# Gated delta attention with a mixture of experts on one core: moments, gathers and running products traced earlier

## The chip, the cores and the metric

The kernel runs on one core of a Trainium2 chip. The metric is device time in microseconds of one execution, the median of several runs. The engines are named as in the profile: PE is TensorE, DVE is VectorE, ACT is ScalarE, POOL is GpSimd, and SP is SyncE, which here only issues DMAs.

## What is computed

The block normalises x and adds to it an attention layer and a mixture of experts. All numbers are float32; x has 2 batches of 2048 tokens of 512.

```python
xn = _layernorm(x)                                   # (2, 2048, 512)
# attention: 16 heads of 128
q, k, v = (silu(causal_dwconv(xn @ W, cw, cb)) for each of q, k, v)   # 4 taps, k scaled by 128 ** -0.5
alpha, beta = sigmoid(xn @ Wa + ba), sigmoid(xn @ Wb + bb)            # one per token and head
def step(S, qt, kt, vt, at, bt):                     # over the 2048 tokens
    err = S @ kt - vt
    S = at * S - bt * outer(err, kt)
    return S, S @ qt
attn = (norm_per_head(o) * ln_w + ln_b) * sigmoid(xn @ Wg) @ Wo
# experts: the first 512 tokens, each to 4 of 16, sorted by expert
ffn = scatter_add(w * (silu(xs @ gate) * (xs @ up)) @ down)
return x + attn + ffn
```

## The kernel before

The recurrence over tokens is done in chunks of C = 128 tokens. Inside a chunk the triangular system is solved with products of small matrices, and a state S of 128x128 per head goes from chunk to chunk. Four chunks make a block (BLK = 512 tokens, CB = 4); a batch has NBK = 4 blocks or NC = 16 chunks. Heads go in pairs (HG = 2), so a batch has NP = 8 pairs and the program 16 units u, each a pair of heads of one batch.

**Before the recurrences.** norm(b) takes x in four groups of four chunks. For a group it loads four tiles xin (four buffers), computes mean and variance on DVE (L370, L371), adds eps (ve, L373), and raises to the power -0.5 on POOL (rs, L375). Each chunk is then normalised on DVE (xn, L384), transposed on PE (L390), copied by ACT, and multiplied by the weights of alpha and beta (L393). At the end norm computes the decays and writes them to memory: a_d (alpha per token) and gin_d. norm(0) runs first, then route, which sorts the tokens by expert. The two first units' keys (keys(0), keys(1), called from firsts) follow, and between them the generator norm(1) is stepped once from the 13th step on, and projection(0) at steps 20, 23, 26 and 29.

**keys(u)** has eight items (four blocks of two heads) of two steps each, a step being what runs up to a yield. The first step projects (L149, four matmuls in one of two PSUM banks "p"), and convolves: ACT copies the bank (raw, L131) and forms the last tap with the bias (cv, L135), POOL copies three columns of halo (L130, L133), DVE adds three taps (L137), ACT applies Silu to give kf (L139). The second step multiplies each chunk of kf with itself (L201) into a bank (the bank "o" in firsts, a bank "p" in the recurrences), builds the decays decA with four ACT operations (L209), turns them into running products with a scan on DVE (L213) whose multiplier is row, the alphas of the item broadcast to all partitions by a DMA (ask, L182), and multiplies both (aTf, L215). The tile row has one buffer; the next item's is asked for behind aTf. The first row of a unit is asked for when keys(u) starts.

**inverses(u)** computes 32x32 inverses on POOL in 30 rounds of a product and a sum (L243, L246). For unit 0 it is drained at once, between keys(0) and keys(1); for later units a round is handed out at three of the six ticks.

**recurrence(b)** walks the 128 chunks of a batch, and two more steps to drain. A step m has six ticks. In each, before (chunk m: the inverse of 128x128), after (chunk m-1: the state) and output (chunk m-2) are stepped; projection of the next block (q, v, g) at ticks 1 and 4, keys(u + 2) at ticks 0 and 3, the experts at ticks 2 and 5:

```python
if tick in (1, 4):
    step(nxt)
if tick in (0, 3):
    step(ks)
step(last)
if tick in (2, 5):
    step(ex)
```

So a unit's keys fill eight of its sixteen steps. **experts** is one generator over 31 tiles of 128 tokens; its first step gathers tokens (xg) and three parts of weights (w) by indirect DMAs on POOL (L900), the next transposes xg on PE (L920) and copies it to xgT (L922).

**What sets the order.** The text gives the traced order. The framework's scheduler then places each instruction on its engine's queue by its own model of time, with the traced order as priority, and derives all waits. Two calls in keys (keep_in_program_order on the decays and on the scan) hold these behind what was traced before them on their engine. Tiles of one tag share a fixed number of buffers.

Of the kernel before, what the change touches and what calls it, by code (L numbers as in the profile page):

```python
# [7 lines left out]
F32 = mybir.dt.float32  # L8
I32 = mybir.dt.int32
AF = mybir.ActivationFunctionType  # L10
ALU = mybir.AluOpType
# [3 lines left out]
P = 128  # L15
NB, T, HID = 2, 2048, 512
# [7 lines left out]
HG = 2  # L24
# [18 lines left out]
def block_kernel(ctx, tc, x, wq, wk, wv, wg, wo, wa, wb, ba, bb, par, consts,  # L43
# [9 lines left out]
    def bank(pool, tag):  # L53
        return pool.tile([P, 512], F32, tag=tag, name=tag)
# [104 lines left out]
    def load_wk(u):  # L159
        if u < NB * NP and u not in wks:  # L160
            wks[u] = load_w(ap, "wk", wk, u % NP * HG, f"wk{u}")

    def keys(u, xts, bank_k=(ps_p, "p")):

        b, hp = divmod(u, NP)
        h0 = hp * HG
        load_wk(u)
        w = wks[u]
        if u == NP:
            bt[b] = beta_of()
            nc.sync.dma_start(out=bt[b], in_=bt_d)
        n = CB * DW

        def ask(blk, h):  # L180
            row = ap.tile([P, n], F32, tag="row", name="row")
            nc.sync.dma_start(  # L182
                out=row, in_=a_d[b][h0 + h, blk * n:(blk + 1) * n].partition_broadcast(P))
            return row

        row = ask(0, 0)
        for blk in range(NBK):
            xt = xts(b, blk)
            for h in range(HG):
                ps = proj(w, h, xt)  # L190
                kt = ap.tile([P, BLK], F32, tag="kf", name="kf", bufs=2)
                conv_silu(ps, 1, h0, h, blk, kt)
                if (blk, h) == (NBK - 1, HG - 1):
                    if u + 1 != NP + 2:
                        load_wk(u + 1)
                nc.sync.dma_start(out=k_d[u][blk][h], in_=kt)
                yield
                pk = bank(*bank_k)
                for c in range(CB):
                    a = kt[:, c * C:(c + 1) * C]  # L200
                    nc.tensor.matmul(pk[:, c * C:(c + 1) * C], lhsT=a, rhs=a, start=True, stop=True)  # L201
                aT = ap.tile([P, CB, C], F32, tag="aTf", name="aTf", bufs=2)

                dec = ap.tile([P, CB, DW], F32, tag="decA", name="decA", bufs=2)
                for c in range(CB):
                    ci = blk * CB + c
                    tc.keep_in_program_order(nc.scalar.activation(  # L209
                        dec[:, c, :], unit, AF.Identity, scale=bt[b][:, ci, h0 + h:h0 + h + 1]))  # L210
                flat = dec.rearrange("p c j -> p (c j)")
                tc.keep_in_program_order(
                    nc.vector.tensor_tensor_scan(flat, row, flat, 0.0, ALU.mult, ALU.add))  # L213
                nc.sync.dma_start(out=dec_d[b][hp][blk][:, h * n:(h + 1) * n], in_=flat)
                nc.vector.scalar_tensor_tensor(  # L215
                    aT, pk.rearrange("p (c j) -> p c j", c=CB), -1.0 / D, dec[:, :, 0:C],
                    ALU.mult, ALU.mult)
                if (blk, h) != (NBK - 1, HG - 1):
                    row = ask(blk + (h + 1) // HG, (h + 1) % HG)
                o = h * NC + blk * CB  # L220
                nc.sync.dma_start(out=aT_d[u][:, o:o + CB, :], in_=aT)
                yield
# [124 lines left out]
    with ExitStack() as es:  # L347
# [11 lines left out]
        np_ = es.enter_context(tc.tile_pool(name="norm", bufs=2))  # L359
        def norm(b):  # L360
            psg = bank(ps_l, "l")
            for g in range(NBK):
                xin = [np_.tile([P, HID], F32, tag="xin", name="xin", bufs=4) for _ in range(CB)]
                for i in range(CB):
                    c = g * CB + i
                    nc.sync.dma_start(out=xin[i], in_=x[b, c * C:(c + 1) * C, :])
                mv = np_.tile([P, CB, 2], F32, tag="mv", name="mv")
                for i in range(CB):
                    st = np_.tile([P, 6], F32, tag="st", name="st")
                    nc.vector.bn_stats(st, xin[i])  # L370
                    nc.vector.bn_aggr(mv[:, i, :], st)  # L371
                ve = np_.tile([P, CB], F32, tag="ve", name="ve")
                nc.vector.tensor_scalar(ve, mv[:, :, 1], EPS, None, ALU.add)  # L373
                rs = np_.tile([P, CB], F32, tag="rs", name="rs")
                nc.gpsimd.tensor_tensor(rs, ve, mhalf[:, 0:CB], ALU.pow)  # L375
                if b == 0:
                    xt = xT[b, g] = xp.tile(
                        [P, NKT, BLK], F32, tag="xT", name=f"xT{b}_{g}", bufs=NBK)
# [93 lines left out]

        def firsts():
            for u in range(2):
                for _ in keys(u, get_xT, (ps_o, "o")):
                    yield
                if u == 0:
                    drain(inverses(0))
                    yield

        f0, p0, n1 = firsts(), projection(0), norm(1)
        for i, _ in enumerate(f0):
            if i > 12:
                next(n1, None)
            if i in (20, 23, 26, 29):
                next(p0)
# [23 lines left out]
    for t in [*ops[0].values(), *ops[1].values(), *invs]:  # L510
        nc.gpsimd.memset(t, 0.0)
    ex = experts(nc, bank, ps_p, half, k2, ident, wrow, trow, xn_d, y_d, (ew0, ew1, ew2), (ewd0, ewd1))
    def before(n, c):

        u, blk = blocks[n]
# [153 lines left out]
    def recurrence(b, first):  # L669
# [21 lines left out]
        for m, at in enumerate([*steps, None, None]):  # L691
# [30 lines left out]
            for tick in range(6):  # L722
# [8 lines left out]
                if tick in (0, 3):  # L731
                    step(ks)
                step(last)
                if tick in (2, 5):
                    step(ex)
                if inv and at and ci > 0:
                    if tick == 1:
# [274 lines left out]
```

## Time and profile before

| | |
|---|---|
| median of 3 runs | 4071.16 us (4069.39 to 4077.14) |
| the profiled execution's own time | 4071.89 us |
| its span, first to last instruction | 4070.1 us |
| mean granted clock of PE | 0.988 |
| busy: PE, DVE, ACT, POOL | 3825.9, 2337.3, 1642.1, 1822.5 us |
| DVE waiting for rows (the scan, L213) | 9.2 us in 9 cases |
| mean of a scan, of aTf, of a power 128x4 | 1380, 681, 1072 ns |
| DMA, mean over the span | 133 GB/s |

The page has a line for each engine in 40 slices of about 102 us: a digit is the busy share in tenths. A view of waits has, for each engine and line, whom it waited for, the total, the number of cases and the longest. A line of a timeline has start, duration, engine, line of the source, operation, output and inputs with their form and the number of instructions merged, and in square brackets the idle time just before with what ended it. The busy time of PE is modelled, and a wait with several causes is put down to the last of them.

### The profile page before, as it was taken

The numbers are of one execution on the slowest core, as the hardware profiler recorded it, in microseconds if no ns is written. First come the engines' busy times: TensorE is split into PE (matmuls) and PEld (weight loads), VectorE is DVE, ScalarE is ACT, GpSimd is POOL, SyncE is SP. The second block draws the span as 40 slices with busy tenths as digits, with TensorE's granted clock in tenths as the row PEclk, the third lists the DMA queues.
The fourth block names the chain that finished last, engine by engine and source line by source line (L and its number), as shares of the span: only waits on it lengthen the run. The fifth ranks groups of instructions, "written<-read, shape, count | busy, mean of one in ns | idle before, by whom it ended". The sixth has DMA issues, their size and how long they took to land.

```text
span 4070.1 us, 58930 instructions
## 1 busy us (share of the span) xinstructions
PE 3825.9 (94%) x18046; PEld 2463.9 (61%) x18046; DVE 2337.3 (57%) x6132; ACT 1642.1 (40%) x4025; POOL 1822.5 (45%) x3496
## 2 busy tenths in 40 slices
PE   8679999999999999999989999999999999999999
PEld 6356666666666666666654456666666666666554
DVE  6555565564655557676751056767676767666321
ACT  3344344443444435454530044545454545444210
POOL 1436556464564645454550045455454545472100
PEclk9889999999999999999999999999999999999999
DMA  4555555455555454354564344334443434424322
GB/s 148 158 150 166 164 161 164 148 162 152 161 160 160 147 148 130 108 151 117 174 200 124 106 128 118 108 116 113 113 119 107 120 107 123 123 75 121 100 94 78
DMA packets 579705, 541.36 MB, mean 133 GB/s; under 512 B 354688, under 2 KB 421760, under 8 KB 574272
## 3 DMA queue, kind: packets, MB, share of 16 engines
q1 hardware_dynamic: 557280, 456.18, 38.2%
q0 software_dynamic: 22112, 81.41, 6.5%
q8 instruction: 147, 2.41, 0.2%
q14 instruction: 166, 1.36, 0.1%
HBM read 363.69 MB, written 173.67 MB: 132 GB/s over the span
## 4 chain that ended last, share of the span: by engine, by line
PE 45%; DVE 12%; POOL 6%; ACT 5%; issue 2%; DMA 1%; SPq 0%; POOLq 0%; ACTq 0%; DVEq 0%
PE p L149 20%; PE p L781 11%; DVE cv L137 7%; POOL rs L643 2%; ACT cv L135 2%; PE c L615 2%; PE c L606 2%; POOL qg L311 2%; PE l L536 1%; PE o L629 1%; PE c L596 1%; PE o L632 1%; ACT raw L131 1%; PE p L932 1%; DVE o L657 1%
## 5 line engine op out<-in xcount | busy, mean ns | idle before, releaser
L137 DVE SCALAR_TENSOR_TENSOR cv<-raw,prm,cv 128x512 f32<-128x512 f32 x1152 | 921.8, 800 | 307.4 <-ACT cv L135 289.2
L131 ACT COPY raw<-p 128x512 f32<-128x512 f32 x384 | 223.2, 581 | 784.0 <-PE p L149 762.5
L149 PE MATMUL p<-xT,wv 128*128 128x512 f32 x1024 | 480.3, 596 | 4.6 <-DVE xgT L922 4.5
L149 PE MATMUL p<-xT,wq 128*128 128x512 f32 x1024 | 476.5, 595 | 7.4 <-DVE aTf L215 5.1
L149 PE MATMUL p<-xT,wg 128*128 128x512 f32 x1024 | 473.5, 594 | 3.9 <-ACT cv L135 3.5
L781 PE MATMUL p<-wo,oTf 128*128 128x512 f32 x1024 | 455.0, 596 | 1.2 <-DMA oTf<-oT_d 1.1
L149 PE MATMUL p<-xT,wk 128*128 128x512 f32 x896 | 417.2, 604 | 36.8 <-DVE aTf L215 29.7
L657 DVE TENSOR_SCALAR o<-o,mv,rs 128x128 f32<-128x128 f32 x512 | 194.8, 404 | 237.7 <-POOL rs L643 237.7
L781 PEld LDWEIGHTS p<-wo,oTf 128*128 128x128 f32 x1024 | 191.2, 192 | 219.5 <-issue 216.5
L643 POOL TENSOR_TENSOR rs<-rs,mhalf 128x2 f32<-128x2 f32 x256 | 229.0, 894 | 203.2 <-DVE rs L642 196.0
L565 POOL COPY inv<-iT 32x32 f32<-32x32 f32 x512 | 137.7, 269 | 386.9 <-DVE top L560 254.9
L133 POOL COPY halo<-raw 128x3 f32<-128x3 f32 x288 | 70.7, 245 | 528.3 <-ACT raw L131 523.5
L135 ACT ACTIVATE cv<-p,prm 128x512 f32<-128x512 f32 x384 | 301.0, 784 | 0.2
L550 POOL TENSOR_TENSOR kg<-kv,gd 128x256 f32<-128x256 f32 x256 | 177.6, 694 | 274.3 <-ACT kv L548 268.3
L243 POOL TENSOR_TENSOR t<-Y 128x30 f32<-128x30 f32 (+14 forms) x480 | 278.0, 579 | 38.2 <-DMA dec_d<-decA 0.2
L246 POOL TENSOR_TENSOR Y<-Y,t 128x30 f32<-128x30 f32 (+14 forms) x480 | 276.0, 575 | 36.5
L149 PEld LDWEIGHTS p<-xT,wk 128*128 128x128 f32 x896 | 161.3, 192 | 193.8 <-issue 154.4
L559 DVE STREAM_TRANSPOSE iT<-l 128x32 f32<-128x32 f32 x256 | 55.4, 216 | 382.4 <-PE l L557 382.3
L149 PEld LDWEIGHTS p<-xT,wq 128*128 128x128 f32 x1024 | 179.2, 191 | 156.2 <-issue 147.6
L149 PEld LDWEIGHTS p<-xT,wg 128*128 128x128 f32 x1024 | 179.6, 191 | 155.5 <-issue 150.2
L149 PEld LDWEIGHTS p<-xT,wv 128*128 128x128 f32 x1024 | 178.2, 191 | 145.6 <-issue 139.7
L606 PEld LDWEIGHTS c<-r,inv 128*128 128x128 f32 x960 | 140.1, 191 | 148.3 <-issue 66.1
(176 smaller groups left out, 7423.4 us busy)
## 6 DMA issues: line engine op xcount, KB each, us to landing
row<-a_d SPq DMA_DIRECT2D x128, 258.0 KB
dec_d<-decA SPq DMA_DIRECT2D x128, 258.0 KB
decB<-dec_d SPq DMA_DIRECT2D x64, 516.0 KB
k_d<-kf SPq DMA_DIRECT2D x128, 256.0 KB
gin<-gin_d SPq DMA_DIRECT2D x128, 256.0 KB
k<-k_d SPq DMA_DIRECT2D x64, 512.0 KB
aT_d<-aTf SPq DMA_DIRECT2D x128, 256.0 KB
oT_d<-oT SPq DMA_DIRECT2D x256, 128.0 KB
```

Of the source, the lines that this page charges most:

```text
L131: nc.scalar.copy(raw[:, KS - 1:], ps)
L135: nc.scalar.activation(cv, ps, AF.Identity, bias=cbias(p, h0 + h), scale=tap(p, h0 + h, KS - 1))
L137: nc.vector.scalar_tensor_tensor(cv, raw[:, j:j + BLK], tap(p, h0 + h, j), cv, ALU.mult, ALU.add)
L149: nc.tensor.matmul(ps, lhsT=w[:, k, h * D:(h + 1) * D], rhs=xt[k], start=(k == 0), stop=(k == NKT - 1))
L243: nc.gpsimd.tensor_tensor(t, bass.AP(col.tensor, col.offset, [col.ap[0], (Q, j), (0, n)]), bass.AP(row.tensor, row.offset, [row.ap[0], (0, ...
L246: nc.gpsimd.tensor_tensor(Y[:, 0:j, j + 1:], Y[:, 0:j, j + 1:], t, ALU.add)
L550: nc.gpsimd.tensor_tensor(kg, kv[:, 0], bcast(gd1[b][:, ci, hs], D), ALU.mult)
L565: nc.gpsimd.tensor_copy(inv[0:Q, h, Q:2 * Q], iT[r + Q:r + 2 * Q])
L606: nc.tensor.matmul(pw[:, h * D:(h + 1) * D], lhsT=inv[:, h, :], rhs=r[:, h, :], start=True, stop=True)
L643: nc.gpsimd.tensor_tensor(rs, rs, mhalf[:, 0:HG], ALU.pow)
L657: nc.vector.tensor_scalar(o[:, h, :], po[:, h * D:(h + 1) * D], mv[:, h, 0:1], rs[:, h:h + 1], ALU.subtract, ALU.mult)
L781: nc.tensor.matmul(py, lhsT=oT[:, h, :], rhs=wos[h], start=(h == 0), stop=(h == H - 1))
```

## The change

It has four parts. (1) norm(1) computes the moments of all four groups ahead: firsts steps it at steps 1, 3, 5 and 7 as well, each time loading a group of x and taking its statistics; at step 13 one power of 16 columns gives all 16 chunks' factors, and the groups of x are loaded a second time to be normalised. norm(0) keeps its order. (2) The generator of the experts gets its first step right after the memsets ahead of the recurrences, and step m = 0 of each recurrence no longer steps it. (3) In keys the decays, the scan and their store move from the second step of an item to the end of the first, behind the convolution; the second step keeps the products and aTf. (4) The row of the next item is asked for right behind the scan, and the last item of a unit asks for the first row of the next unit; the very first is asked for ahead of keys(0).

```diff
@@ -160,6 +160,15 @@
         if u < NB * NP and u not in wks:
             wks[u] = load_w(ap, "wk", wk, u % NP * HG, f"wk{u}")
 
+    rows = {}
+
+    def ask(u, blk, h):
+        if u < NB * NP:
+            rows[u, blk, h] = row = ap.tile([P, CB * DW], F32, tag="row", name="row")
+            nc.sync.dma_start(
+                out=row, in_=a_d[u // NP][u % NP * HG + h, blk * CB * DW:(blk + 1) * CB * DW]
+                .partition_broadcast(P))
+
     def keys(u, xts, bank_k=(ps_p, "p")):
 
 
@@ -177,13 +186,6 @@
             nc.sync.dma_start(out=bt[b], in_=bt_d)
         n = CB * DW
 
-        def ask(blk, h):
-            row = ap.tile([P, n], F32, tag="row", name="row")
-            nc.sync.dma_start(
-                out=row, in_=a_d[b][h0 + h, blk * n:(blk + 1) * n].partition_broadcast(P))
-            return row
-
-        row = ask(0, 0)
         for blk in range(NBK):
             xt = xts(b, blk)
             for h in range(HG):
@@ -194,12 +196,6 @@
                     if u + 1 != NP + 2:
                         load_wk(u + 1)
                 nc.sync.dma_start(out=k_d[u][blk][h], in_=kt)
-                yield
-                pk = bank(*bank_k)
-                for c in range(CB):
-                    a = kt[:, c * C:(c + 1) * C]
-                    nc.tensor.matmul(pk[:, c * C:(c + 1) * C], lhsT=a, rhs=a, start=True, stop=True)
-                aT = ap.tile([P, CB, C], F32, tag="aTf", name="aTf", bufs=2)
 
 
 
@@ -210,13 +206,19 @@
                         dec[:, c, :], unit, AF.Identity, scale=bt[b][:, ci, h0 + h:h0 + h + 1]))
                 flat = dec.rearrange("p c j -> p (c j)")
                 tc.keep_in_program_order(
-                    nc.vector.tensor_tensor_scan(flat, row, flat, 0.0, ALU.mult, ALU.add))
+                    nc.vector.tensor_tensor_scan(flat, rows.pop((u, blk, h)), flat, 0.0, ALU.mult, ALU.add))
                 nc.sync.dma_start(out=dec_d[b][hp][blk][:, h * n:(h + 1) * n], in_=flat)
+                m = blk * HG + h + 1
+                ask(u + m // (NBK * HG), m // HG % NBK, m % HG)
+                yield
+                pk = bank(*bank_k)
+                for c in range(CB):
+                    a = kt[:, c * C:(c + 1) * C]
+                    nc.tensor.matmul(pk[:, c * C:(c + 1) * C], lhsT=a, rhs=a, start=True, stop=True)
+                aT = ap.tile([P, CB, C], F32, tag="aTf", name="aTf", bufs=2)
                 nc.vector.scalar_tensor_tensor(
                     aT, pk.rearrange("p (c j) -> p c j", c=CB), -1.0 / D, dec[:, :, 0:C],
                     ALU.mult, ALU.mult)
-                if (blk, h) != (NBK - 1, HG - 1):
-                    row = ask(blk + (h + 1) // HG, (h + 1) % HG)
                 o = h * NC + blk * CB
                 nc.sync.dma_start(out=aT_d[u][:, o:o + CB, :], in_=aT)
                 yield
@@ -359,20 +361,43 @@
         np_ = es.enter_context(tc.tile_pool(name="norm", bufs=2))
         def norm(b):
             psg = bank(ps_l, "l")
-            for g in range(NBK):
+
+            def moments(mv, xs):
+                for i, a in enumerate(xs):
+                    st = np_.tile([P, 6], F32, tag="st", name="st")
+                    nc.vector.bn_stats(st, a)
+                    nc.vector.bn_aggr(mv[:, i, :], st)
+
+            def power(mv, n):
+                ve = np_.tile([P, NC], F32, tag="ve", name="ve")
+                nc.vector.tensor_scalar(ve[:, 0:n], mv[:, :, 1], EPS, None, ALU.add)
+                rs = np_.tile([P, NC], F32, tag="rs", name="rs")
+                a = mhalf[:, 0:1]
+                nc.gpsimd.tensor_tensor(
+                    rs[:, 0:n], ve[:, 0:n], bass.AP(a.tensor, a.offset, [a.ap[0], (0, n)]), ALU.pow)
+                return rs
+
+            def load(g):
                 xin = [np_.tile([P, HID], F32, tag="xin", name="xin", bufs=4) for _ in range(CB)]
                 for i in range(CB):
                     c = g * CB + i
                     nc.sync.dma_start(out=xin[i], in_=x[b, c * C:(c + 1) * C, :])
-                mv = np_.tile([P, CB, 2], F32, tag="mv", name="mv")
-                for i in range(CB):
-                    st = np_.tile([P, 6], F32, tag="st", name="st")
-                    nc.vector.bn_stats(st, xin[i])
-                    nc.vector.bn_aggr(mv[:, i, :], st)
-                ve = np_.tile([P, CB], F32, tag="ve", name="ve")
-                nc.vector.tensor_scalar(ve, mv[:, :, 1], EPS, None, ALU.add)
-                rs = np_.tile([P, CB], F32, tag="rs", name="rs")
-                nc.gpsimd.tensor_tensor(rs, ve, mhalf[:, 0:CB], ALU.pow)
+                return xin
+
+            if b > 0:
+                mvs = np_.tile([P, NC, 2], F32, tag="mvs", name="mvs", bufs=1)
+                for g in range(NBK):
+                    moments(mvs[:, g * CB:(g + 1) * CB, :], load(g))
+                    yield
+                rss = power(mvs, NC)
+            for g in range(NBK):
+                xin = load(g)
+                if b == 0:
+                    mv = np_.tile([P, CB, 2], F32, tag="mv", name="mv")
+                    moments(mv, xin)
+                    rs = power(mv, CB)
+                else:
+                    mv, rs = (a[:, g * CB:(g + 1) * CB] for a in (mvs, rss))
                 if b == 0:
                     xt = xT[b, g] = xp.tile(
                         [P, NKT, BLK], F32, tag="xT", name=f"xT{b}_{g}", bufs=NBK)
@@ -472,6 +497,8 @@
 
         def firsts():
             for u in range(2):
+                if u == 0:
+                    ask(0, 0, 0)
                 for _ in keys(u, get_xT, (ps_o, "o")):
                     yield
                 if u == 0:
@@ -480,7 +507,7 @@
 
         f0, p0, n1 = firsts(), projection(0), norm(1)
         for i, _ in enumerate(f0):
-            if i > 12:
+            if i > 12 or i in (1, 3, 5, 7):
                 next(n1, None)
             if i in (20, 23, 26, 29):
                 next(p0)
@@ -510,6 +537,7 @@
     for t in [*ops[0].values(), *ops[1].values(), *invs]:
         nc.gpsimd.memset(t, 0.0)
     ex = experts(nc, bank, ps_p, half, k2, ident, wrow, trow, xn_d, y_d, (ew0, ew1, ew2), (ewd0, ewd1))
+    next(ex)
     def before(n, c):
 
         u, blk = blocks[n]
@@ -731,7 +759,7 @@
                 if tick in (0, 3):
                     step(ks)
                 step(last)
-                if tick in (2, 5):
+                if tick in (2, 5) and m != 0:
                     step(ex)
                 if inv and at and ci > 0:
                     if tick == 1:
```

## Prediction

> **What bounds it now.** I read the page first: its head, and the slices of part 2.
>
> ```profile
> span 4070.1 us, 58930 instructions
> PE 3825.9 (94%) x18046; PEld 2463.9 (61%) x18046; DVE 2337.3 (57%) x6132; ACT 1642.1 (40%) x4025; POOL 1822.5 (45%) x3496
> ...
> PE   8679999999999999999989999999999999999999
> ```
>
> TensorE (PE) is busy for 94%, so the most that better order can win is its idle time, 4070.1 - 3825.9 = 244 us. Four fifths of the run are nines; slices 1 to 3 (0 to 305 us) are not. The change moves no matmul out of the program, so I ask only which idle time it can fill. Next, the view of waits for PE, total us, times and longest:
>
> ```profile
> PE c L390 <- DVE xn L384: 44.3, 4, 25.2
> PE p L149 <- DVE aTf L215: 41.6, 43, 1.9
> ...
> PE p L920 <- DMA xg<-xn_d,trow: 10.8, 1, 10.8
> ...
> PE p L932 <- DVE aTf L215: 5.7, 8, 1.2
> ...
> PE o L201 <- DVE aTf L215: 4.8, 2, 3.2
> ...
> PE p L946 <- DVE aTf L215: 2.5, 3, 1.1
> ```
>
> Three causes, and the change touches each. The timeline of the 25.2 us wait (DVE, then POOL, then PE):
>
> ```profile
> 178.50 0.33 DVE L373 TENSOR_SCALAR ve<-mv 128x4 f32<-128x4 f32 x1
> 205.59 1.00 DVE L384 TENSOR_SCALAR xn<-xin,mv,rs 128x512 f32<-128x512 f32 x2 [26.75 <-POOL rs L375]
> ...
> 202.68 1.89 POOL L252 COPY X<-Y 128x1024 f32<-128x1024 f32 x1
> 204.53 1.02 POOL L375 TENSOR_TENSOR rs<-ve,mhalf 128x4 f32<-128x4 f32 x1
> ...
> 206.19 1.97 PE L390 MATMUL c<-unit,xn 128*128 128x128 f32 x8 [25.16 <-DVE xn L384]
> ```
>
> ve is ready at 178.8; its power of 1.02 us runs at 204.5, because POOL is inside the 60 operations of inverses(0) from 165.0 to 204.6. DVE holds at xn, and PE behind it. The third group's chunks are the victims. The steady stage, one step of the second recurrence:
>
> ```profile
> 2630.22 2.33 DVE L213 TENSOR_TENSOR_SCAN decA<-row,decA 128x516 f32<-128x516 f32 x1
> 2633.09 0.41 DVE L657 TENSOR_SCALAR o<-o,mv,rs 128x128 f32<-128x128 f32 x1 [0.54 <-POOL rs L643]
> 2633.41 0.68 DVE L215 SCALAR_TENSOR_TENSOR aTf<-p,decA 128x512 f32<-128x512 f32 x1
> ...
> 2634.15 3.27 PE L149 MATMUL p<-xT,wk 128*128 128x512 f32 x7 [1.28 <-DVE aTf L215]
> ```
>
> The products of L201 (2627.0 to 2628.1) hold one of two p banks until aTf has read them; the scan stands in front of aTf, and the next projection waits 1.28 us for the bank.
>
> [...] DVE idled 26.75 us while the convolution behind xn (206.5 to 209.5), whose halo copy I take to be that of 161.8, needed nothing more from POOL. [...] granted clock 0.81, 0.60 and 0.79 in the three 25 us from 200, where PE was busy 18.55, 18.15 and 13.20 us. [...] The scan agrees: 1.225 us as a rule, 2.33 above, where POOL's qg (2630.20, 1.27 us) had started first.
>
> **Part one, moments.** Removed: batch 1's four powers become one. Its 16-column form is in no row; four columns take 1.015 us, two 0.70 undisturbed, so 0.16 a column: 1.015 + 12 x 0.16 = 2.9 us; bounds 1.0 (flat) and 4.1 (four of the old). It is traced at step 13, ahead of inverses(0), so no xn waits behind the chain. That frees at most 25.2 us, and the fourth group's 2.98 at 227.7 (PE L390 waiting for xn). What is late next: POOL's raw<-halo at 205.51, still behind the chain, whose consumer ran at 228.0 and would now want it at 203. The chain stretches when DVE works: the rows up to the 220-wide pair took 14.6 us beside a busy DVE (164.97 to 179.61), the same widths on the way down 11.7 (190.92 to 202.61) beside an idle one, 25% more; its 25.7 us left at 178.9 may become 32. So 0 to 8 us come back; I take 4: 25.2 - 4 = 21. With 3 for the fourth group and 4 of clock: at most 50 us busy x (1 - 0.73) = 13, of which most is latency behind other engines, so a third. Sum 28.
>
> Added: 16 loads of x, 256 KB each; 16 x 0.39 us of SP's queue, 4.2 MB, or 15 us of all DMA at 275 GB/s, the highest slice I saw there, in a stretch whose DMA share is 0.62 to 0.81. On SP k_d, dec_d, row and aT_d stand behind a load that waits for one of four xin buffers; the scans and the later loads of k and decB wait for those. The statistics of three groups, 12 x (0.68 + 0.17) = 10.2 us, move from 130, 171 and 211 into the first keys, where DVE is busy 22.2 of 25 us (75 to 100) and then 18.4 and 16.0. The work is moved, not added, and PE has about 3 us of free time in each window, so the cost is 0 to 10; I take 4. **Part one: -24.**
>
> **Part two, gathers.** The three weight gathers already ran at 70.8 to 74.6; only xg's is late: it follows the memsets at 262.1 and PE stands in front of L920 from 255.3 to 266.1. The gather does not get sooner, since its tile and the memsets need the freed pools; what helps is that step m = 0 no longer asks for its transposes. PE then takes the wk projection (ran at 268.0) at once, and L529 (ran at 272.98) when the memsets and puts of 256 to 261 have landed, by about 263. Gain 10.8 + 0.8 (the wait for xgT) at most; the expert's transposes come a step later with no idle time. At least 6, if L529 is held by the puts. **Taken: -9.**
>
> **Part three, scans.** The four waits for aTf come to 54.6 us in 56 cases, 0.98 each, 49.8 of it in the recurrences. Without the scan aTf is ready 1.23 (or 2.33) sooner, more than the mean: I count 45 of the 49.8 gone. What takes its place, in the step above: kf's Silu ends at 2625.46, the four decA of 0.32 follow on ACT to 2626.7, the scan to 2627.95. On ACT the raw and cv of the next projection stand behind (cv would end at 2627.9 instead of 2626.6; PE takes that bank at 2628.16: just in time). On DVE the convolution of that projection (2626.65) and xs (2627.32) stand behind the scan: xs goes to 2628.2, and PE's L576, which ran at 2627.93, comes 0.3 later. Not every step is so tight, so I take 0.15 us for each of 112 items: 17. From both sides: 0 if the scan falls into DVE's idle time (DVE is busy 70% there), 1.23 x 112 = 138 if PE feels each. Net 45 - 17 = 28. In the first keys, on the o bank, 4.8 us and part of ACT's 26 us at kf (it waits for L201) go: 4. Rows: the scans' waits for them, 9.2 us in nine cases, are all there; one buffer stays, so inside a group the lead is one item as before, and only a group's first row gains: 0 taken, 0 to 9 possible. **Part three: -32.**
>
> **Sum.** -24 - 9 - 32 = -65. The profiled execution took 4071.9 us around its span of 4070.1, 0.7 above the median of the runs: 4071.9 - 65 = 4006.9, and on the runs' scale 4006.
>
> **Rivals.**
> - *The wait on POOL moves.* raw<-halo behind the chain holds DVE instead of the power: part one gives 3, not 24: 4027. For it: POOL still serves the chain first. Against: that copy's consumer has 20 us of other work ahead of it.
> - *Part three is given back* by xs, the convolution or r (PE already waits 29.8 us for r L600): 4034. With the first rival too, 4055.
> - *Slower.* The scan now stands ahead of what PE asks for next in each item. In place of 17 us it costs up to 138: 4006 + 121 = 4127. The turn is at 17 + 65 = 82 us, 0.73 us per item. For it: DVE in the step above runs without a gap from 2626.65 to 2632.5. Against: kf is ready 1.5 us before L201, and PE's queue there holds 3.6 us of projection.
> - *It does not do what it says*: the engines' order is the scheduler's, so the power may still be placed late, and each trace order reshuffles all: within 8 us of before.
>
> **Numbers.** 0.2% of the time, 8 us, is about what a measurement of this kernel can tell from no change. Near 4006 (3985 to 4020): 0.50. First rival 0.15, second 0.14, both 0.03, better than all of it (whole waits and rows gone, clock held, about 3975) 0.05: faster 0.87. Same 0.05. Slower 0.08. The range from 3972 to 4056 leaves out about 0.16.
>
> **What would show it.** Right: no PE wait at L390 above 3 us; one power of 128x16, before the chain; no wait for xg; PE waits for aTf below 10 us in all; mean scan shorter than 1380 ns; PE busy unchanged near 3826 us. Wrong: DVE or PE idle over 10 us between 170 and 215 behind POOL's copies; waits for xs L570, r L600 or ACT cv L135 grown by over 30 us; PE's share below 94%.

## The result, and the profile after

The change made the kernel slower: 4093.95 us (4079.1 to 4101.23) against 4073.97 us (4061.22 to 4086.08) of the kernel before, 20 runs each, a ratio of 1.0047 with a 95% interval from 1.0037 to 1.0057. The forecast was 4006 us. The profiled execution took 4099.78 us around its span of 4098.0. The head of its page:

```profile
span 4098.0 us, 58897 instructions
...
PE 3835.0 (94%) x18046; PEld 2465.8 (60%) x18046; DVE 2303.5 (56%) x6129; ACT 1648.0 (40%) x4024; POOL 1830.0 (45%) x3493
...
PE   8779999999999999999989999999999999999999
```

PE does the same 18046 matmuls in nearly the same busy time (3835 against 3826 us), so 19 of the 28 us more of span are idle time of PE. The other 9 us go with a lower granted clock, 0.984 in the mean against 0.988. The view of waits for PE says what it stood for:

```profile
PE l L604 <- DVE xs L598: 47.9, 28, 4.3
PE c L634 <- DVE r L628: 39.1, 50, 1.0
PE c L415 <- DVE xn L409: 37.3, 3, 21.0
PE p L149 <- ACT cv L135: 15.7, 14, 2.1
```

The wait of L149 for aTf (41.6 us before, 0.4 now) and that for xg (10.8) are gone, as they should be. But the wait for xs was 16.0 us before (L576 for L570) and is three times that, r was 29.8, cv was 5.2, and the wait for xn lost only 7 of its 44 us. In these names top, bot, inv and xs are pieces of the inverse of chunk m, r and w belong to the state of chunk m-1, oT to the output of chunk m-2. Two places show why the waits grew.

**The start.** The timeline of the changed kernel where xn used to wait for the power (SPq are DMAs issued by SP):

```profile
114.66 3.35 POOL L376 TENSOR_TENSOR rs<-ve,mhalf 128x16 f32<-128x16 f32 x1
...
203.31 1.84 DVE L137 SCALAR_TENSOR_TENSOR cv<-raw,prm,cv 128x512 f32<-128x512 f32 x2 [11.33 <-POOL raw L130]
...
209.21 0.32 SPq L256 DMA_DIRECT2D X_d<-Y  x1
...
211.54 2.25 SPq L384 DMA_DIRECT2D xin<-in_x  x4
...
215.32 0.55 DVE L409 TENSOR_SCALAR xn<-xin,mvs,rs 128x512 f32<-128x512 f32 x1 [10.18 <-DMA xin<-in_x]
...
215.93 1.11 PE L415 MATMUL c<-unit,xn 128*128 128x128 f32 x4 [20.95 <-DVE xn L409]
```

The power is now one of 16 columns, and it runs 50 us ahead of inverses(0). The stall has only changed its name. SP issued nothing from 178.69 to 209.21: its next instruction is the store of inverses(0), and the second load of xin stands behind it. In the view of waits for SP the longest wait of X_d (L256) for POOL's Y is 30.5 us; POOL's last Y ends at 209.2, the two stores follow at 209.21 and 211.16, and the four loads of xin behind them at 211.54. Ahead of that, POOL's copy of the halo (L130), which ran at 203.09 inside the inverses, held DVE for 11.33 us.

**The steady stage.** One step of the second recurrence, like the one that the prediction shows:

```profile
2659.51 0.63 ACT L139 ACTIVATE kf<-cv 128x512 f32<-128x512 f32 x1 [1.88 <-DVE cv L137]
...
2660.05 1.27 ACT L205 ACTIVATE decA<-unit,bt 128x129 f32<-128x129 f32 x4
...
2660.42 0.39 PE L596 MATMUL l<-top,a 128*128 128x128 f32 x2
...
2661.34 1.35 DVE L209 TENSOR_TENSOR_SCAN decA<-row,decA 128x516 f32<-128x516 f32 x1 [1.10 <-ACT decA L205]
...
2662.36 0.44 ACT L592 COPY bot<-iT 32x32 f32<-32x32 f32 x2
...
2662.80 0.27 DVE L598 COPY xs<-l 128x128 f32<-128x128 f32 x1
...
2663.22 0.46 PE L604 MATMUL l<-bot,xs 128*128 128x128 f32 x2 [1.52 <-DVE xs L598]
```

L596 has written what xs copies by 2660.8. But the scan stands ahead of xs on DVE, and it stands there idle for 1.10 us until the four decays are done; xs runs 2 us late and PE waits 1.52 us. On ACT bot and inv stand behind the same decays. Over the whole run DVE stands idle at the scan for its decays 48.7 us, in 61 of the 128 items. The price can be read off the waits for PE between the outputs of chunks 128 and 207 (keys run in 40 of these 80 chunks). Before, then after:

```profile
PE p L149 <- DVE aTf L215: 16.3, 19, 1.5
PE c L606 <- DVE r L600: 14.5, 20, 0.9
PE c L606 <- POOL Y L246: 6.0, 10, 0.9
```

```profile
PE c L634 <- DVE r L628: 20.0, 25, 1.0
PE l L604 <- DVE xs L598: 12.4, 8, 1.6
...
PE p L149 <- ACT cv L135: 5.1, 5, 1.2
PE l L604 <- ACT oT L692: 4.2, 4, 1.1
PE l L604 <- ACT inv L601: 3.6, 3, 1.6
PE c L643 <- ACT w L637: 2.6, 10, 0.3
```

Gone are 16.3 (aTf) and 4.9 (Y, of which 1.1 is left), 21.2 us or 0.53 per item; new are 12.4 + 5.5 (r) + 5.1 + 4.2 + 3.6 + 2.6 = 33.4 us or 0.84 per item. The difference, 12.2 us, is most of the 13.4 us that the stretch lost (987.7 us against 974.3).

### The profile page after: what moved, and what is told of

Same layout as the page of the kernel before. It is cut to its first block, busy times and chain, and to the rows that moved or that the text cites. A ratio compares the mean times of both kernels' runs of the same rounds, so it can differ in the third digit from the quotient of the medians.

```text
span 4098.0 us, 58897 instructions
## 1 busy us (share of the span) xinstructions
PE 3835.0 (94%) x18046; PEld 2465.8 (60%) x18046; DVE 2303.5 (56%) x6129; ACT 1648.0 (40%) x4024; POOL 1830.0 (45%) x3493
## 3 DMA queue, kind: packets, MB, share of 16 engines
q14 instruction: 166, 1.36, 0.1%
## 4 chain that ended last, share of the span: by engine, by line
PE 48%; DVE 17%; ACT 7%; POOL 5%; DMA 4%; issue 3%; SPq 1%; ACTq 0%; POOLq 0%; DVEq 0%
PE p L149 21%; PE p L809 10%; DVE cv L137 10%; PE p L960 2%; PE l L564 2%; ACT cv L135 2%; PE c L643 2%; ACT decA L205 2%; PE c L634 2%; POOL qg L313 2%; POOL rs L671 2%; DVE o L685 1%; PE c L624 1%; ACT raw L131 1%; DVE decA L209 1%
## 5 line engine op out<-in xcount | busy, mean ns | idle before, releaser
L149 PE MATMUL p<-xT,wv 128*128 128x512 f32 x1024 | 487.2, 603 | 21.6 <-ACT cv L135 10.4
L149 PE MATMUL p<-xT,wg 128*128 128x512 f32 x1024 | 475.7, 596 | 5.1 <-ACT cv L135 2.1
L149 PE MATMUL p<-xT,wq 128*128 128x512 f32 x1024 | 478.8, 596 | 0.0
L149 PE MATMUL p<-xT,wk 128*128 128x512 f32 x896 | 417.6, 605 | 7.8 <-ACT cv L135 3.2
L248 POOL TENSOR_TENSOR Y<-Y,t 128x30 f32<-128x30 f32 (+14 forms) x480 | 315.0, 656 | 37.0
L133 POOL COPY halo<-raw 128x3 f32<-128x3 f32 x288 | 88.4, 307 | 523.1 <-ACT raw L131 519.7
L593 POOL COPY inv<-iT 32x32 f32<-32x32 f32 x512 | 140.1, 274 | 407.3 <-DVE top L588 251.0
L578 POOL TENSOR_TENSOR kg<-kv,gd 128x256 f32<-128x256 f32 x256 | 186.2, 727 | 265.9 <-ACT kv L576 260.2
L671 POOL TENSOR_TENSOR rs<-rs,mhalf 128x2 f32<-128x2 f32 x256 | 184.1, 719 | 214.2 <-DVE rs L670 208.9
L149 PEld LDWEIGHTS p<-xT,wv 128*128 128x128 f32 x1024 | 179.2, 193 | 164.5 <-issue 138.3
L149 PEld LDWEIGHTS p<-xT,wg 128*128 128x128 f32 x1024 | 180.1, 191 | 158.2 <-issue 151.3
L149 PEld LDWEIGHTS p<-xT,wq 128*128 128x128 f32 x1024 | 179.3, 192 | 144.7 <-issue 144.5
L149 PEld LDWEIGHTS p<-xT,wk 128*128 128x128 f32 x896 | 163.2, 194 | 164.6 <-issue 154.2
```

The source lines that it names most:

```text
L149: nc.tensor.matmul(ps, lhsT=w[:, k, h * D:(h + 1) * D], rhs=xt[k], start=(k == 0), stop=(k == NKT - 1))
L248: nc.gpsimd.tensor_tensor(Y[:, 0:j, j + 1:], Y[:, 0:j, j + 1:], t, ALU.add)
L578: nc.gpsimd.tensor_tensor(kg, kv[:, 0], bcast(gd1[b][:, ci, hs], D), ALU.mult)
L593: nc.gpsimd.tensor_copy(inv[0:Q, h, Q:2 * Q], iT[r + Q:r + 2 * Q])
L671: nc.gpsimd.tensor_tensor(rs, rs, mhalf[:, 0:HG], ALU.pow)
```

## The experiments

Sixteen kernels, each with five rounds beside the kernel before. "First scores" is the start of the first matmul of the first recurrence, a mark of the start only, since what PE has done by then differs a little between kernels; "stretch" the time between the stores of the outputs of chunks 128 and 207; the last columns are PE's waits for xn and for the 128-wide xs (xs L570 before, L598 after). These four columns are from one profile each; e7 and e15, whose program is the same up to the first recurrence, show the scatter of a start (239.6 and 243.7). Times in us.

| run | ratio to before, 95% interval | first scores | stretch | xn | xs |
|---|---|---|---|---|---|
| before | 1 | 273.0 | 974.3 | 44.3 | 16.0 |
| the change | 1.0047 (1.0037 to 1.0057) | 264.4 | 987.7 | 37.3 | 47.9 |
| e1 third part alone | 1.0031 (1.0022 to 1.0040) | 266.2 | 987.7 | 41.4 | 44.7 |
| e2 parts one and two | 1.0005 (0.9996 to 1.0014) | 273.0 | 974.8 | 39.2 | 20.3 |
| e3 part one alone | 1.0009 (0.9999 to 1.0019) | 270.4 | 973.4 | 38.8 | 15.2 |
| e5 decays alone ahead | 1.0018 (1.0010 to 1.0026) | 276.0 | 977.5 | 41.7 | 18.8 |
| e6 scan behind xs | 0.9928 (0.9913 to 0.9944) | 268.7 | 965.2 | 40.9 | 16.4 |
| e4 third part, no pins | 0.9869 (0.9850 to 0.9887) | 265.6 | 963.3 | 39.6 | 23.5 |
| e10 third part, decays not pinned | 0.9942 (0.9923 to 0.9960) | 261.7 | 974.0 | 39.8 | 19.6 |
| e9 before, no pins | 0.9859 (0.9845 to 0.9874) | 271.3 | 961.6 | 45.4 | 23.5 |
| e7 part one, stores later | 0.9930 (0.9912 to 0.9947) | 239.6 | 973.4 | 21.1 | 15.9 |
| e8 the same, inverses in rounds | 0.9956 (0.9942 to 0.9970) | 249.1 | 973.8 | 17.2 | 16.5 |
| e13 the change, no pins | 0.9885 (0.9870 to 0.9900) | 268.2 | 963.1 | 34.9 | 27.4 |
| e14 the change, stores later | 1.0014 (1.0002 to 1.0025) | 254.4 | 986.2 | 26.6 | 53.4 |
| e11 both, the whole change | 0.9833 (0.9821 to 0.9846) | 255.6 | 964.1 | 23.4 | 28.9 |
| e12 both, without part two | 0.9843 (0.9831 to 0.9856) | 262.2 | 964.0 | 24.2 | 23.7 |
| e15 pins in first keys only, one part | 0.9828 (0.9815 to 0.9841) | 243.7 | 961.6 | 21.0 | 24.1 |
| e16 the same with part two | 0.9808 (0.9794 to 0.9821) | 243.2 | 961.3 | 21.0 | 28.8 |

### Which part loses

**e1**, the third part alone:

```diff
-            if i > 12 or i in (1, 3, 5, 7):
+            if i > 12:
-    next(ex)
-                if tick in (2, 5) and m != 0:
+                if tick in (2, 5):
```

(and norm(1) takes its moments group by group, as before.)

> The third part alone: decays and scan behind the convolution and the row of the next unit asked ahead, with the moments and the experts as before. Theory A (the third part costs): the scan and its four decays stand ahead of the xs copy and of r in the recurrence, some 0.25 us lost for each of the 112 items of keys there: about +25 to +38 us against the kernel before, PE's wait of the L604 matmuls for xs L598 at 40 us or more, and the loss growing by about 2 us per unit between the first and the last keys. Theory B (the third part gains its 30 us and the loss is of part two, whose expert matmuls and gathers stand earlier in the recurrences): -15 to -35 us and no wait of more than 20 us for xs.

Measured: 4089.03 us against 4077.2. The loss is smaller than theory A had it (12 us, not 25), but the sign and the wait for xs are theory A's, and the stretch is that of the whole change to a tenth. From the stores of chunk 128 to the end this run lost 13.9 us, the change 13.5.

**e2**, parts one and two, and **e3**, part one alone. Both undo the move in keys:

```diff
                 nc.sync.dma_start(out=k_d[u][blk][h], in_=kt)
-                dec = ...  (decays, scan, store, ask)
                 yield
                 pk = bank(*bank_k)
                 ...
+                dec = ...  (decays, scan, store)
                 nc.vector.scalar_tensor_tensor(aT, ...)
+                ask(...)   (the next row, if it is of the same unit)
```

> The change without its third part: decays and scan back in the second step of an item of keys, beside the key products; moments and experts as in the change. Theory A (the third part costs): the start keeps the 11 us that it gained and the recurrences lose nothing: -8 to -16 us against the kernel before; the wait of PE for aTf is back at 40 to 50 us and that for xs falls to some 16 us. Theory B (part two costs): 0 to +35 us against the kernel before, with the loss growing through both recurrences.

> The first part alone: moments of the second batch beside the first keys, one power of sixteen; experts, decays and scan as before. Theory A (the stall before xn only moved, from the power behind the inverses to raw behind the inverses and to the second load of xin): -3 to -12 us against the kernel before, the 25 us wait for xn replaced by one of some 10 us for the xn of a late xin and one of about 10 us of DVE for the copy of the halo. Theory B (the moments gain the predicted 24 us and something else of the change eats it): -18 to -28 us.

Measured: 4080.29 and 4079.26 us against 4077.2; neither is told apart from the kernel before. So theory A was right that the recurrences lose nothing without part three (974.8 and 973.4), and wrong that the start keeps 11 us: by the first scores it keeps 0 to 2.6. The sooner first scores of the change came with part three (266.2 us in e1). Part one, forecast at -24 us, is worth nothing as it stands; part two is worth nothing beside it. PE does wait a little less: its idle time in the profiles is 237.2 (e2) and 240.0 us (e3), against 244.2 before. But the granted clock is lower, in the mean of the runs 0.9845 and 0.9844 against 0.9855, and in the 67 runs of the kernel before 0.001 of clock goes with about 3.5 us, so that by this estimate the one about takes back the other.

### Where part three loses

**e5**: as e1, with the decays where the change has them and the scan back behind the key products:

```diff
-                tc.keep_in_program_order(nc.vector.tensor_tensor_scan(...))   (and its store)
                 ask(u + m // (NBK * HG), m // HG % NBK, m % HG)
                 yield
                 ...
                 aT = ap.tile([P, CB, C], F32, tag="aTf", name="aTf", bufs=2)
+                tc.keep_in_program_order(nc.vector.tensor_tensor_scan(...))   (and its store)
```

> The third part split: on ACT the four decays stand behind the convolution as in the change, on DVE the scan stays in the second step ahead of aTf; moments and experts as before. If DVE's scan ahead of xs is what costs: within 8 us of the kernel before, or a few us faster, since aTf no longer waits for the decays; the wait for xs at 15 to 22 us. If the decays on ACT ahead of bot, inv and cv are what costs: +15 to +35 us, with the wait for xs or for ACT's copies grown as in the change.

Measured: 4084.49 us, 7.3 us more than before, with the wait for xs at 18.8 us, as the first guess had it. This is not a loss by waiting: PE's idle time in the profile is 239.0 us (244.2 before), and in the stretch 45.0 (45.4 before). What is longer is PE's busy time, 3839.9 us against 3825.9, and the granted clock is lower: 0.977 to 0.982 in all 22 runs, 0.983 to 0.989 in all 67 of the kernel before. Why this order has the lower clock is open. PE's waits in the stretch show what the place of the decays does:

```profile
PE c L633 <- DVE r L627: 19.2, 25, 1.0
PE p L149 <- DVE aTf L219: 7.7, 15, 0.8
PE l L603 <- ACT bot L591: 5.9, 10, 0.9
```

The wait for aTf has halved, but bot has become a wait that was not there, and r has grown from 14.5 to 19.2. So the early decays on ACT take back what they bring; the net loss of e1 needs the scan ahead of xs as well.

**e6**: an item of keys in the recurrences gets a third step, so that decays and scan come behind xs of the same chunk:

```diff
                 nc.sync.dma_start(out=k_d[u][blk][h], in_=kt)
+                if three:
+                    yield
                 dec = ...  (decays, scan, store, ask; yield; products and aTf)
-                if tick in (0, 3):
+                if tick in (0, 3, 4):
                     step(ks)
```

> The third part alone, but an item of keys in the recurrences has three steps: convolution, then (three ticks later, behind the xs copy of the chunk) decays and scan, then the key products and aTf. The scan still ends well before aTf asks for it, and no longer stands on DVE ahead of the xs copy of the same chunk. If the place of the scan ahead of xs is what costs: the wait for xs back to 15 to 22 us, the stretch between the outputs of chunks 128 and 207 back to 972 to 977 us (987.7 with the scan ahead alone, 974.3 before), the whole within 6 us of the kernel before or faster. If a scan and decays earlier on DVE and ACT cost wherever they stand: that stretch at 983 to 990 us and the whole +8 to +18 us.

Measured: 4045.51 us against 4077.68, 32 less, with the wait for xs at 16.4 us and that for aTf on L149 down to 9.2. The stretch, 965.2 us, is better than either theory said. So the move of decays and scan ahead of aTf does bring what was forecast for it; only their place ahead of xs took that back.

**e4**: as e1, but the scheduler may place decays and scan. **e10**: as e1, decays free, scan pinned. **e9**: the kernel before, both free, nothing moved:

```diff
-                    tc.keep_in_program_order(nc.scalar.activation(
-                        dec[:, c, :], unit, AF.Identity, scale=bt[b][:, ci, h0 + h:h0 + h + 1]))
+                    nc.scalar.activation(
+                        dec[:, c, :], unit, AF.Identity, scale=bt[b][:, ci, h0 + h:h0 + h + 1])
-                tc.keep_in_program_order(
-                    nc.vector.tensor_tensor_scan(flat, row, flat, 0.0, ALU.mult, ALU.add))
+                nc.vector.tensor_tensor_scan(flat, row, flat, 0.0, ALU.mult, ALU.add)
```

> The third part alone, without the pins that keep decays and scan in program order: the planner then puts the scan of an item between o and the first copy of xs (32 wide), one item earlier, and xs L597 keeps the place that it had. If the place ahead of xs is what costs: wait for xs under 25 us, the stretch between the outputs of chunks 128 and 207 at 972 to 979 us. If an early scan only moves the loss to the next instruction behind it: waits for pT, r or top grown by 10 us or more and that stretch at 980 to 990 us.

> The third part alone, scan still pinned and the four decays not: ACT then runs the decays behind inv and cv, and DVE's scan comes behind the xs copy too. If the pinned decays are what pushes the scan and ACT's copies into the way of xs: the gain of the unpinned run within 15 us (4022 to 4037 us). If the pin of the scan is what counts: 4070 to 4095 us, as with both pinned.

> The kernel before with nothing moved: only the pins on decays and scan are gone, so that the planner places them; on DVE the scan then comes between o and the 32-wide xs copy, as in the unpinned run of the third part. If the place on the engines is all that counts: within 10 us of that run (4022 us), -45 to -60 us against the kernel before. If the scan must be written ahead of the key products for the planner to find the place in time: 0 to -25 us, with 25 us or more of PE's wait for aTf left.

Measured: 4021.68, 4054.69 and 4022.24 us. e9 settles it: with nothing moved in the text, the gain is 57 us, as large as that of e4 (56). The timeline of e9:

```profile
2583.55 1.28 ACT L211 ACTIVATE decA<-unit,bt 128x129 f32<-128x129 f32 x4 [1.83 <-DVE aTf L216]
...
2584.87 1.39 DVE L214 TENSOR_TENSOR_SCAN decA<-row,decA 128x516 f32<-128x516 f32 x1
2590.21 0.63 ACT L139 ACTIVATE kf<-cv 128x512 f32<-128x512 f32 x1 [1.88 <-DVE cv L137]
2592.16 0.39 PE L593 MATMUL l<-top,a 128*128 128x128 f32 x2
...
2592.70 0.28 DVE L595 COPY xs<-l 128x128 f32<-128x128 f32 x1
2593.28 0.39 PE L601 MATMUL l<-bot,xs 128*128 128x128 f32 x2
...
2607.13 0.63 ACT L139 ACTIVATE kf<-cv 128x512 f32<-128x512 f32 x1 [1.87 <-DVE cv L137]
```

The scan needs only row and the decays, nothing of kf. Left free, decays and scan run more than an item ahead. Counted from the first item, the scan shown is the 94th and so belongs to the 94th Silu, that at 2607.13; the one at 2590.21 is the 93rd. The decays start as soon as an aTf has left one of the two buffers of decA: in the same timeline an aTf ends at 2595.89, and the next four decays start at 2595.93. In the recurrences the scan starts 26 us before its own item's Silu (median). xs follows L593 at once, and L601 has no wait. Freeing the decays alone (e10) brings 36 of the 66 us between e1 and e4, by the ratios. The pinned scan still stands ahead of xs, and in 36 of the 48 items of the second recurrence ahead of top as well, but DVE never stands idle there for the decays (48.7 us after the change); PE waits for xs 19.6 us and for top 28.5 us in 53 cases (9.6 in 18 after the change). e10 lies between its two guesses; the pins act together.

### Where part one's gain stayed

**e7**: part one alone; the first inverses are traced in rounds, so that their stores are traced last:

```diff
                 for _ in keys(u, get_xT, (ps_o, "o")):
+                    next(inv, None)
+                    next(inv, None)
                     yield
                 if u == 0:
-                    drain(inverses(0))
+                    inv = inverses(0)
+                    next(inv)
                     yield
+            drain(inv)
```

Up to the end of the inverses this changes no order on POOL's queue, only on SP's. **e8** hands out three rounds a step, and the first of the three waits for kf:

```diff
                 conv_silu(ps, 1, h0, h, blk, kt)
+                mark["kf"] = kt[:, 0:1]
...
-                    next(inv, None)
-                    next(inv, None)
+                    for _ in range(3):
+                        give(inv, mark.pop("kf", None))
```

> The first part alone, with the first inverses traced in rounds between the steps of the second unit's keys: POOL's order stays as it is with the first part alone, but on SP the stores of the inverses come after all loads of xin and no longer hold them back. If the late load of xin behind these stores is what kept the gain of the moments: wait for xn down from 39 us to 28 us or less, the first scores of the recurrence 8 to 15 us earlier than with the moments alone (270 us), the whole -4 to -14 us against the kernel before. If POOL's copy of the halo behind the inverses holds the same chain anyway: within 4 us of the moments alone, which is -3 to +6 us against the kernel before.

> As the run with the inverses stored later, and each third round of the inverses also waits for the convolution of the second unit's keys (a copy of one column of kf into its scratch tile, as the recurrence does it), so that POOL takes the copies of the halo and the rounds in turn. If the copy of the halo behind the inverses is the second half of the stall: DVE's wait for raw falls from 11 us to 4 us or less and the first scores come at 250 to 260 us, -8 to -18 us for the whole against the kernel before. If the stall only moves on to the store of the inverses, now later: the first scores at 268 us or later, and PE waits there for what is loaded from the inverses.

Measured: 4046.74 and 4058.92 us against 4077.68. e7's gain of 31 us is over twice the guess. The stall in e3, and then the timeline of e7:

```profile
208.77 0.55 DVE L410 TENSOR_SCALAR xn<-xin,mvs,rs 128x512 f32<-128x512 f32 x1 [20.68 <-DMA xin<-in_x]
```

```profile
169.80 3.68 SPq L385 DMA_DIRECT2D xin<-in_x  x4
...
182.61 1.11 PE L416 MATMUL c<-unit,xn 128*128 128x128 f32 x4 [4.91 <-DVE xn L410]
...
221.74 0.38 SPq L257 DMA_DIRECT2D X_d<-X  x1
```

All four loads of xin are issued at 169.8; in e3 one is, and the next at 205.4 (in the change all four at 211.5). PE's longest wait for xn there is 4.91 us instead of 17.55 (20.95), and the first scores come 31 us sooner than in e3. POOL's copy of the halo comes no sooner (193.5, and 193.9 in e3), yet DVE waits for it in neither: in e3 the copy is done 15 us before the xn at which DVE stands, and in e7 DVE has xn to do meanwhile. So with part one alone the stall is that of the late loads; of the runs shown so far only the change, with part three, has DVE at raw too. Of e7's 31 us, 24 are idle time of PE (220.6 us); the rest goes with a granted clock of 0.990 in the mean of its runs against 0.985. Taking the inverses in rounds (e8) is 12 us slower than e7, though against the kernel before it comes out about as guessed (19 us faster, first scores at 249.1): X is ready at 214.0 instead of 207.8, and PE waits up to 9.3 us for aTf in the first keys.

### The whole change with each thing undone, and both

**e13** is the change without pins, **e14** the change with the stores later, **e11** has both, **e12** both without part two.

> The whole change with one thing undone: the pins on decays and scan. If the pinned place of decays and scan is what turned its gain into a loss: 4020 to 4030 us (4022 for the third part without pins, parts one and two worth nothing as they stand), 60 us or more under the change. If something else of the change loses the time in the recurrences: 4060 us or more.

> The whole change with one thing undone: the stores of the first inverses come after the loads of xin on SP, pins as in the change. If the late second load of xin is what kept part one's gain: 4060 to 4074 us (4094 less 20 to 33), the wait for xn down to 30 us or less. If the copy of the halo behind the inverses holds the start in any case: within 8 us of the change.

> The whole change with its two faults taken away: decays and scan not pinned, and the first inverses traced in rounds so that their stores come after the loads of xin on SP. If the two causes are apart from each other and part two is worth nothing: 4077 - 55 - 30 = 3992 us, within 10 us, which is -75 to -95 us against the kernel before. If both gains are the same idle time counted twice: 4010 to 4025 us.

> As the run with both faults taken away, without part two: the experts' first gathers come where they came before. If part two is worth nothing: within 5 us of that run. If the forecast for part two was right: 7 to 11 us slower than it, with a wait for xg of some 10 us back at the start of the first recurrence.

Measured: 4027.52, 4083.33, 4009.95 and 4016.53 us. The pins alone turn the change from 1.0047 to 0.9885. The stores alone bring less than expected, 13 us by the ratios instead of 20 to 33: the first scores come at 254.4, and with the scans ahead in the first keys DVE still stands 9.2 us at raw. The sum of both, 68 us, missed the expected 85, and likely for the same reason: the start comes at 255.6 and not at 240, with 11.5 us at raw.

**e15** keeps the pins, and the scan in the second step, in the first keys alone (with part one and the stores later); **e16** adds part two.

```diff
-    def keys(u, xts, bank_k=(ps_p, "p")):
+    def keys(u, xts, bank_k=(ps_p, "p"), pin=lambda i: i):
-                for _ in keys(u, get_xT, (ps_o, "o")):
+                for _ in keys(u, get_xT, (ps_o, "o"), tc.keep_in_program_order):
```

> Part one with the stores later, scan written in the second step as before, and pinned in the first keys alone; the planner places it in the recurrences. The start is that of the run with the stores later (first scores at 240 us), the recurrences those of the unpinned kernel before. If the unpinned scan in the first keys is what spoilt the sum of the two gains: 4077 - 30 - 50 = 3997 us, within 8 us, under the run with both faults taken away (4010 us). If the recurrences can't be faster because of what they share: 4008 to 4016 us.

> As the run with pins in the first keys alone, with part two. If part two is worth what was forecast: 7 to 11 us faster than that run; if nothing: within 5 us of it.

Measured: 4005.22 and 3998.73 us against 4075.47. The start is back at 243 us and the recurrences are those of e9. e16 is faster than both kernels, by 1.9% (1.8 to 2.1) than the one before; its span is 3997.7 us with PE busy for 3820.9, so PE's idle time is 177 us instead of 244. Part two is worth 6.6 us in one pair (e12, e11) and 6.5 in the other (e15, e16); in each the intervals overlap, but every run of e16 (3993.2 to 4000.7 us) is below every run of e15 (4002.3 to 4009.1), so it is likely. Beside the pinned keys it was worth nothing (e3, e2: 1 us the other way).

## Why the prediction was wrong

Two terms failed. The cost of part three, sized at 17 us, came to more than its whole gain; and the 24 us of part one stayed out, held back by a wait on SP's queue for which the sum had no term.

- **What bounds it: right.** The three waits that it named are those that can be won: e16 has 67 us less idle time of PE, near the 65 forecast, by another order. The waits for aTf on L149 and for xg are gone there and that for xn is down to 21.0 us, while that for xs has grown to 28.8. That the sum agrees so well is in part luck.
- **Part one, -24, came to nothing (e3).** The wait was read rightly, and its size is near what can be won once the loads have room (e7, 24 us of idle time, 31 in all). The step that failed is "What is late next": it names raw behind the chain and takes 4 us for it. Measured in e3: 20.68 us of DVE at xn for the second load of xin, and no wait for that copy. In the change: 11.33 us at raw, then 10.18 for xin. The prediction counted what stands behind the new loads on SP, but never asked what the new loads stand behind: the stores of the inverses, which wait for POOL. The first rival (the wait on POOL moves to raw) is half of what happened in the change and none of it in e3; SP's queue no rival named. The clock, taken as a gain of 4 us by the author's estimate from three windows, was no gain in the profiles of the change and of e1 to e3 (0.982 to 0.985 against 0.988). The power took 3.35 us where 2.9 was taken.
- **Part two, -9:** the wait for xg went as forecast. The time did not, with the pins; with the other faults gone it is about -6.5, inside its 6 to 11.6.
- **Part three, -32, came to +12 (e1).** The gain was sized well: of the 49.8 us for aTf in the recurrences, of which it counted 45, about 1 is left. The 4 us of the first keys did not come: PE waits there for aTf 8.5 us (4.8 before). The term that failed is "I take 0.15 us for each of 112 items". Measured in the second recurrence: 0.84 per item, against a gain of 0.53. It was taken from one step in which kf's Silu ended 1.36 us ahead of L568, so that the scan would hardly wait; in the step shown above it ends 0.28 us ahead of L596, and DVE stands at the scan for 1.10 us with xs behind it. It also priced xs and cv alone, where r, bot, inv, oT and w came later too. The rival on the slower side had the right mechanism; its turn, 0.73 us per item, still counted on the gains of the other parts (without them it is 45 us, or 0.40 per item). For the first recurrence no such price was taken apart; there the waits for xs come to 23.0 us in 11 cases up to the output of chunk 63.
- **The order is the scheduler's**: this rival took it for harmless. The pins were in the code that the prediction described, and it didn't ask what they forbid. That was the larger lever: 57 us without moving a line.
- **Signs.** Right: one power of 128x16 ahead of the chain, no wait for xg, aTf on L149 near nothing, mean scan 1296 ns instead of 1380. Wrong: a PE wait of 20.95 us for xn. PE's busy time, 3835 us, was 9 above. Of the three signs for a wrong forecast two came, DVE idle over 10 us behind POOL's copy and the wait for xs grown by 32 us; PE's share stayed at 94%.

What stays open: why the granted clock differs between these orders; why e1 is worse by 0.3% and the change by 0.5% when parts one and two are worth nothing alone (the difference, 0.0016, is about as large as the two intervals allow; the idle times of PE in the profiles, 257.3 and 263.0 us, differ by 5.7), and how much of the gain of the free scan is left in its waits for row (24.3 us of DVE's idle time in 12 cases in e9).

## What to carry to other kernels

Before moving an instruction earlier, ask on each queue that it lands on what it will stand behind and what will stand behind it, SP's queue for its loads included; here the loads of xin stood behind a store that waited for POOL and were issued at 211.54, where with the stores later they were issued at 169.80 (e7). In this kernel a producer off the critical path did well behind the instruction for which PE is waiting next (e6, a ratio of 0.9928 to before), and better as early as its own inputs allow (e9, 0.9859), but not just ahead of that instruction (e1, 1.0031). Where a scheduler places the instructions, first look at what it has been forbidden: taking the pins away gained 57 us with nothing moved, where the order made by hand lost 20.

## What the hardware showed

- POOL's power of 128x16, in its one case, took 3.35 us, and that of 128x4 1.015 us in the median of eight in the kernel before: by these two an estimate of 0.19 us for each further column, where 0.16 was worked out from the forms of two and four.
- The scan of 516 columns took 1.225 us in the median of its 128 cases in the kernel before (1.216 to 2.33), the product of 512 columns behind it (aTf) 0.680 in the median of the 112 in the recurrences: a ratio of 1.8.
- The order of the other engines goes with another granted clock of PE: 0.977 to 0.982 in the runs of e5, 0.983 to 0.987 in those of the kernel before beside e7, 0.989 and 0.990 in those of e7. The same 18046 matmuls took PE 3839.9 us in the profile of e5 and 3820.3 in that of e7. So a difference of 10 us between two orders need not be one of waiting.
- DVE was busy 56% of the time and ACT 40% (57 and 40% in the kernel before), and both queues cost PE time all the same, 47.9 us for xs and 15.7 for cv (16.0 and 5.2 before): what counted here was the order of the one queue at the moment, not its load.
